# Moving one batch's preparation, the background's share and the queries' loads in a fused attention and expert kernel

## The chip, the cores and the metric

The kernel runs as one launch on 1 core of one Trainium2 chip. The metric is the device time of that launch in microseconds (us), from the first to the last instruction with what lies around it; lower is better. Engine names in profiles: PE is TensorE (PEld its weight loads), DVE is VectorE, ACT is ScalarE, POOL is GpSimd, SP is SyncE, which here only issues transfers. A trailing q (SPq) marks what an engine's sequencer does.

## What is computed

Input is x of shape (4, 2048, 256): four batches of 2048 tokens. Two blocks follow, each with a norm before and after and a residual.

```python
# block 1: attention with a triangular kernel instead of a softmax, 16 heads of 16 columns
h = layernorm(x)
q, k, v = h @ Wq.T + bq, h @ Wk.T + bk, h @ Wv.T + bv
z_q, z_k = q @ Wproj.T, k @ Wproj.T            # one number per head and token
ctx[i] = sum_j max(0, 1 - |z_q[i] - z_k[j]| / bandwidth[head]) * v[j] / T
x = x + layernorm(ctx)

# block 2: a shared feed-forward and 64 experts, two "halves" of two batches each in the kernel
h = layernorm(x)
shared = (silu(g) * u) @ shared_down * sigmoid(h @ shared_gate)      # g, u = h @ shared_gate_up
w, idx = top_k(softmax(h @ gate_w), 8);  w = w / sum(w)
# each expert takes its first 128 tokens in token order, over all 8192 tokens
y = sum over a token's experts of w * ((silu(g_e) * u_e) @ expert_down[e])
x = x + layernorm(y + shared)
```

The reference sorts z and uses prefix sums for the attention. The kernel evaluates the triangle directly.

## The kernel before

**The loop.** The attention is a hand-ordered loop of 1024 units, 256 for each of the four batches. A unit is one head and one row of 128 keys against all 2048 queries. It makes one score tile of 128 x 2048: `score` computes |q - k| on ScalarE (L1558), or on DVE when DVE has time to spare (L1553 and L1555), and then min(., 1) - 1 on DVE (L1562). `product` multiplies the tile with the values on TensorE (L1588); four units of four heads lie side by side in the array. `evict` takes a finished group of 8 heads out of PSUM. 64 units make a phase: four heads over all 16 rows of keys. The queries of a head are broadcast into a buffer of 128 x 2048 by `load_q` (L1539, two transfers of 512 KB). Before the change the first of the next phase's four heads is loaded at row 11 of 16 of the current phase, and the other three at the first three units of row 15. Query buffers, score tiles and finished groups share a pool of 13 big buffers, taken and given back in order; a score tile's buffer is free once TensorE has read it.

**The background.** All other work is a list of small tasks in the class `Background`: for each an engine, a cost in us, its dependencies and the buffers it takes and gives. After each unit of the loop, `step` emits the tasks whose dependencies are old enough, as long as an engine's cost stays within its share per unit, which is `CAP`. From the start of batch 2 (unit 512) the shares are larger (TensorE 0.88). If a task is needed and is still in the list, `flush` emits it at once. The order that results is fixed when the program is built. After the loop, `drain` emits what is left with a share of 1.0 for every engine.

**What the tasks are, in the order of the list before.** `prepare(i)` for batches 1, 2 and 3, one after the other: load x, norm, transpose, values to `v_d`, and the projection to z with 16 matrices from `m_d` (L436, L442). `finish(b)` once batch b's loop is done: `front` (context and x in, norm, gate), `shared` (the shared feed-forward, L573 and L602, a chunk of 512 tokens at a time) and `tail` (the routing); `stored[b]` lists the stores of the shared result into `y_d`. `finish(0)` waits for the end of `prepare(3)`. When batches 0 and 1 are routed, `all_experts` runs all 64 experts for their tokens: gather (L1041), two matmuls up, one down, and a scatter that adds into `y_d` (L1066).

**The tail.** After the loop: `front_last` for batch 3 (norm, gate, routing), the merge of the second half's tokens, `ranking`, and 15 items of one or two experts each (`item`; their scatters, L1258, add into two copies of `y_d` and wait for `stored[2]`, the stores of batch 2's shared result). What is left of the experts and of batch 2's shared chunks is interleaved, then `shared_last` (L911, L931) and `final`: load y (L1281), for the second half load its second copy and add it (L1288), for batch 3 add the shared result kept in SBUF (L1314), statistics (L1292), a power on POOL (L1298), norm on ScalarE (L1307), and an accumulating store from POOL (L1321). A branch for overflowing experts follows; it is not taken with these inputs.

Of the kernel before, what the change touches and what calls it, by code (L numbers as in the profile page):

```python
# [11 lines left out]
ALU = mybir.AluOpType  # L12
# [13 lines left out]
class Background:  # L26
# [3 lines left out]
           ("dve", "pe"): 1, ("dve", "sp"): 1, ("pool", "dve"): 2, ("dve", "pool"): 1, ("sp", "dve"): 4,  # L30
           ("sp", "pe"): 4, ("sp", "pool"): 4, ("sp", "act"): 5, ("sp", "sp"): 0, ("pool", "sp"): 1,
           ("act", "sp"): 1, ("pe", "sp"): 1}
    CAP = {"pe": 0.84, "dve": 0.65, "act": 0.30, "pool": 1.5, "sp": 2.0}

    def __init__(self, make):
        self.make = make
# [104 lines left out]
def sandwich_kernel(ctx: ExitStack, tc: tile.TileContext, x_in, wqT, bq, wkT, bk, wvT, bv, wprojT, log_bw,  # L141
                    gate_w, sgate_w, sgu_w, sd_w, egu_w, ed_w, out):
    nc = tc.nc
# [53 lines left out]
    def yrows(r0, n, j=0):  # L197

        p, r = part(r0)
        return rows(y_d[p + j], r, n)  # L200
# [25 lines left out]
    with ExitStack() as ph:  # L226
# [14 lines left out]
        def make(tag):  # L241
# [12 lines left out]
                return bigp.tile([P, T], F32, tag=tag, name=f"{tag}_{uid[0]}")  # L254
            return ps.tile([P, BK], F32, tag=tag, name=f"{tag}_{uid[0]}")

        NES, ess = 4, []
        bg = Background(make)
        bg.free["slot"] = [(f"s{i}", 0) for i in range(NSLOT)]
# [196 lines left out]
        def finish(b, after=()):  # L456
# [104 lines left out]
            def shared(c):  # L561
# [32 lines left out]
                for i2 in range(2):  # L594
# [15 lines left out]
                    if i2 == 0:  # L610
# [5 lines left out]
                    a = bg.add("pe", 1.07, lambda f=mmy: f(3), [a], put=acts if i2 == 1 else [], env=env)  # L616
                    yy += [e0, bg.add("dve", 0.45, lambda f=evy: f(1), [a, e0], put=[py], env=env)]
                free_act = a
                free_ys = bg.add("sp", 1.0, lambda ys=ys, r0=r0: nc.sync.dma_start(yrows(r0, CH, 0),
                                                                                   chunkview(env[ys])),  # L620
                                 yy, put=[] if b == NE else [ys], env=env)
# [645 lines left out]
        def final(env, c, deps, more=None, xd=(), tag=""):  # L1267
# [11 lines left out]

            def load(i):  # L1280
                nc.sync.dma_start(yv(i).rearrange("p (n f) -> p n f", n=CH), yrows(r0, CH, i))  # L1281
            l0 = l1 = bg.add("sp", 1.0, lambda: load(0), deps, get={yy: "big" if two else "slot"}, env=env)
            if two:
                l1 = bg.add("sp", 1.0, lambda: load(1), [l0])
            put = [yy]

# [21 lines left out]
                                         scale=rs()[:, i:i + 1])  # L1308
            a = bg.add("dve", 0.0, lambda: None, [l0, l1], get={sm: "v"}, env=env)
            put.append(sm)  # L1310
            if two:
                a = bg.add("dve", 1.25, add, [a])
            if more is not None:
                a = bg.add("dve", 1.25, lambda: nc.vector.tensor_tensor(yv(0), yv(0), more(), ALU.add),  # L1314
# [284 lines left out]
        with tc.manual_schedule():  # L1599
            for n in range(4):  # L1600
                load_q(n)
            for t in range(B * NU + 5):
# [7 lines left out]
                if t == 0:  # L1610
                    for c in range(2, NCH):
                        vts.append(values(env0, c, xt0[c], lambda i, c=c: v0[c * CH + i]))
                    zz = None
                    for q in range(4):
                        for k in range(KF):
                            ts, st = build(1, 4 * q, 4, k, "slot", "dve")
                            zz = accumulate(1, 4 * q, 4, k, ts, zz, st)
                            mst.append(st)
                    last[0] = project(env0, 0, zz, nk0, [1], None)
                    ends = [zz] + [v_[-1] for v_ in vts[1:]]  # L1620

                    def weights():
                        zrow = slot_tile()
                        nc.gpsimd.memset(zrow[:, :TW], 0.0)
                        for i in range(2):
                            nc.sync.dma_start(tab_d[i][TP[i]:TP[i] + P, :], zrow[:, :TW])
                            for j in range(1 + i):
                                nc.sync.dma_start(y_d[i + j][TP[i]:TP[i] + P, :], zrow[:, :F])
                        nc.sync.dma_start(gw[:, :, :E], gate_w.rearrange("(k p) e -> p k e", p=P))
                        with nc.allow_non_contiguous_dma(reason="one gate column"):  # L1630
                            nc.sync.dma_start(gw[:, :, E:E + 1], sgate_w.rearrange("(k p) e -> p k e", p=P))
                        nc.sync.dma_start(sgu, sgu_w.rearrange("(k p) f -> p k f", p=P))
                        nc.sync.dma_start(sd, sd_w.rearrange("(k p) f -> p k f", p=P))
                    bg.add("sp", 3.0, weights, [zz])
                    bg.add("pe", 0.0, lambda: None, ends, put=[("xT", c) for c in range(NCH)],
                           env=env0)
                    last[0] = [last[0]]
                    for i in range(1, B):
                        nks[i], last[i] = prepare(i, after=[last[i - 1]["end"]] if i > 1 else ts[-1:], mdeps=mst)
                if b == 0 and u in (28, 44):  # L1640
                    bg.flush(vts[u // 16 + 1])
                if u == 8 and b > 0:
                    finish(b - 1, after=[last[B - 1]["end"]])
                if u == 0 and b == B - 2:
                    bg.CAP = dict(bg.CAP, pe=0.88, dve=0.75, act=0.4)
                if t == B * NU - 12:
# [2 lines left out]
                if b == 0 and u == 200:  # L1649
                    zt_, z_tag = take("zeros")  # L1650
                    nc.gpsimd.memset(zt_[:, :CH * F], 0.0)
                    zfill = [(1, c) for c in range(NE * NCH, B * NCH)] + [(0, c) for c in range((B - 1) * NCH, B * NCH)]
                if b == 1 and u % 8 == 4 and zfill:
                    i, c = zfill.pop(0)
                    nc.sync.dma_start(yrows(c * CT, CH, i), chunkview(zt_))
# [9 lines left out]
                    bg.flush(last[b + 1]["v"][s:s + 1])  # L1665
                    nc.sync.dma_start(vtile(b + 1, s).rearrange("p a w -> p (a w)"), v_d[b + 1][s])
                if n + 4 < B * H:
                    if s == 11 and j == 0:
                        if ph_ == NU // UP - 1:
                            bg.flush(last[b + 1]["z"])  # L1670
                        if b == 0 and ph_ == 1:
                            bg.flush(last[0])
                        load_q(n + 4)
                    if s == NT - 1 and j < 3:
                        load_q(n + 5 + j)
                was = bg.spent["dve"]
                bg.step()
                spare[0] -= bg.spent["dve"] - was
# [35 lines left out]
            def second(deps, tag):  # L1714
                for c in range(NE * NCH, B * NCH):
                    l = c - (B - 1) * NCH
                    if l < 0:
                        final(env, c, deps, tag=tag)
                    else:
                        final(env, c, deps, lambda l=l: env["ys", l // 2][:, l % 2 * CH * F:(l % 2 + 1) * CH * F],  # L1720
# [69 lines left out]
```

## Time and profile before

| | us |
|---|---|
| median of 3 runs | 2340.97 (2337.17 to 2342.14) |
| profiled execution | 2339.91, of which the span in the trace is 2338.0 |
| loop, first score tile to last | 66 to 2035 |
| first half of the loop (units 0 to 511) | 963.2 |
| second half (units 512 to 1023) | 1005.3 |
| tail | 303 |

The mean granted clock of TensorE is 0.954. A profile page gives busy time, the number of instructions and, in groups, what ended the idle time before them: "112.8 <-DMA qb<-zq_d 57.5" says that the engine stood 112.8 us before these instructions, 57.5 of it until a transfer of queries had landed. Busy time of ScalarE counts overlapping instructions once: 959 score tiles of 1995 ns fill 1837.3 us, that is 1.92 us each. A wait is put down to what came last. An idle engine costs nothing unless others wait for it, and in this loop three engines are nearly full, so each can be the one that others wait for.

### The profile page before, as it was taken

The page shows a single profiled execution, that of the slowest core. Times are in us where ns is not written, and L with a number is a line of the kernel's source. Part 1 is how long each engine was busy: PE and PEld are TensorE (multiplying, and loading weights), DVE is VectorE, ACT ScalarE, POOL GpSimd, SP SyncE. Part 2 cuts the span into 40 slices and gives each one's busy share as a digit, 9 for nine tenths or more (in the row PEclk, how much of TensorE's full clock was granted, in tenths as well). Part 3 has the DMA queues.
Part 4 walks back from the last instruction along what each step waited for, and adds up shares of the span by engine and source line. Part 5 has one row for each costly group of instructions (what it writes and reads, how often), then busy time and mean ns, then how long its engine had stood idle before and what let it go on. Part 6 is the DMA issues. An engine that isn't in the chain of part 4 may idle for free. (4 is left out here: it accounts for less than half of the span.)

```text
span 2338.0 us, 32679 instructions
## 1 busy us (share of the span) xinstructions
PE 1952.5 (84%) x12552; PEld 687.2 (29%) x12552; DVE 1996.1 (85%) x3102; ACT 1966.8 (84%) x1269; POOL 490.4 (21%) x339
## 2 busy tenths in 40 slices
PE   7898979888799899677899887878888889987783
PEld 4332323222223222112222222223332223364342
DVE  4799999898999889999989998989999979886335
ACT  2899999898999998999999998989999989742213
POOL 1001010010120000003200003446553234442463
PEclk9999999999999999989999998999999999988897
DMA  4243534427351202142302014465544243355758
GB/s 127 91 133 120 184 103 153 151 88 264 117 162 64 91 19 70 37 147 69 112 19 81 28 54 122 114 186 151 174 121 136 57 134 90 102 177 147 177 124 197
DMA packets 195078, 274.32 MB, mean 117 GB/s; under 512 B 24833, under 2 KB 165505, under 8 KB 194145
## 3 DMA queue, kind: packets, MB, share of 16 engines
q1 hardware_dynamic: 165680, 235.33, 31.2%
q0 software_dynamic: 23824, 31.70, 8.3%
q10 hardware_dynamic: 5408, 5.11, 0.7%
q8 instruction: 101, 1.65, 0.3%
q14 instruction: 65, 0.52, 0.1%
HBM read 189.18 MB, written 82.90 MB: 116 GB/s over the span
## 5 line engine op out<-in xcount | busy, mean ns | idle before, releaser
L1558 ACT ACTIVATE hat<-qb,nk 128x2048 f32<-128x2048 f32 x959 | 1837.3, 1995 | 112.8 <-DMA qb<-zq_d 57.5
L1588 PE MATMUL pa<-hat,v 128*32 128x512 f32 x8192 | 1115.3, 620 | 284.4 <-DVE hat L1562 272.3
L1562 DVE TENSOR_SCALAR hat<-hat 128x2048 f32<-128x2048 f32 x1024 | 1230.3, 1223 | 97.2 <-ACT hat L1558 91.3
L1588 PEld LDWEIGHTS pa<-hat,v 128*32 128x32 f32 x8192 | 186.2, 110 | 900.0 <-DVE hat L1562 652.6
L1066 POOL DMA_INDIRECT y_d<-s,ix x64 | 147.8, 2309 | 286.7 <-DVE s L1064 145.4
L573 PE MATMUL k<-s,sgu 128*128 128x512 f32 x352 | 198.4, 651 | 0.0
L1041 POOL DMA_INDIRECT s<-tab_d,ix x64 | 106.0, 1657 | 327.6 <-DMA qb<-zq_d 259.0
L499 POOL TENSOR_TENSOR rsc<-rsc,mhalf 128x2 f32<-128x2 f32 x24 | 53.4, 2225 | 521.2 <-DVE rsc L498 521.0
L602 PE MATMUL k<-sd,s 128*128 128x256 f32 x384 | 113.7, 428 | 16.9 <-DVE s L589 7.4
L442 PE MATMUL k<-s,s 128*32 128x512 f32 x768 | 102.4, 592 | 0.0
L602 PEld LDWEIGHTS k<-sd,s 128*128 128x128 f32 x384 | 72.2, 205 | 86.4 <-issue 47.8
L573 PEld LDWEIGHTS k<-s,sgu 128*128 128x128 f32 x352 | 54.8, 192 | 136.3 <-issue 121.2
L305 POOL TENSOR_TENSOR rsa<-rsa,mhalf 128x4 f32<-128x4 f32 x16 | 30.8, 1925 | 290.9 <-DVE rsa L304 285.6
L1553 DVE TENSOR_SCALAR hat<-qb,nk 128x2048 f32<-128x2048 f32 x65 | 83.1, 1279 | 0.1
L1555 DVE TENSOR_SCALAR hat<-hat 128x2048 int32<-128x2048 int32 x65 | 79.9, 1229 | 2.2
L350 PE MATMUL k<-h,s 128*128 128x256 f32 x256 | 73.0, 413 | 0.0
L713 DVE MAX8 codes<-scT 128x8 f32<-128x1152 f32 (+2 forms) x48 | 63.4, 1321 | 0.2
L350 PEld LDWEIGHTS k<-h,s 128*128 128x128 f32 x256 | 45.4, 195 | 54.4 <-issue 48.6
L715 DVE MATCH_REPLACE8 scT<-codes,scT 128x1152 f32<-128x1152 f32 (+2 forms) x44 | 57.6, 1310 | 0.0
L607 DVE TENSOR_SCALAR s<-k,gt 128x256 f32<-128x256 f32 x48 | 22.8, 480 | 36.5 <-PE k L602 32.0
L442 PEld LDWEIGHTS k<-s,s 128*32 128x32 f32 x768 | 31.6, 138 | 54.0 <-issue 53.2
L1258 POOL DMA_INDIRECT y_d<-v,ix x28 | 39.9, 1426 | 23.5 <-DMA y_d<-s 7.9
(319 smaller groups left out, 1643.2 us busy)
## 6 DMA issues: line engine op xcount, KB each, us to landing
qb<-zq_d SPq DMA_DIRECT2D x128, 512.0 KB, 5.5
s<-m_d SPq DMA_DIRECT2D x48, 512.0 KB, 4.8
s<-_attn_hidden_states_dram SPq DMA_DIRECT2D x28, 512.0 KB, 5.5
v_d<-h SPq DMA_DIRECT2D x48, 192.0 KB, 2.6
v<-v_d SPq DMA_DIRECT2D x48, 192.0 KB, 2.5
h<-fn_expert_gate_up_w_dram SPq DMA_DIRECT2D x32, 256.0 KB, 3.5
s<-fn_expert_gate_up_w_dram SPq DMA_DIRECT2D x32, 256.0 KB, 2.8
b<-y_d SPq DMA_DIRECT2D x16, 512.0 KB, 9.3
```

The lines of the kernel that those rows point to most:

```text
L350: nc.tensor.matmul(env[pk][:, i * F:(i + 1) * F], lhsT=xv[:, k, o:o + P], rhs=wv[:, k, :], start=(k == 0), stop=(k == KF - 1))
L442: nc.tensor.matmul(env[pz][c * CR:(c + 1) * CR, :], lhsT=xv[:, r, :], rhs=env[mp][:, k * 2 * F:(k + 1) * 2 * F], start=(r == 0 and k == 0) ...
L573: nc.tensor.matmul(env[p_], lhsT=sgu[:, k, o:o + P], rhs=featview(env[xT])[:, k, :], start=(k == 0), stop=(k == KF - 1))
L602: nc.tensor.matmul(env[py][:, i * F:(i + 1) * F], lhsT=env[acts[f // 2]][:, o:o + P], rhs=sd[:, f, :], start=(f == 0), stop=(f == NI - 1))
L713: a = bg.add("dve", 1.25, lambda c8=c8: nc.vector.max(out=c8, in_=scT[:, :w]), ev + [a])
L1041: g = bg.add("pool", 1.3, lambda: nc.gpsimd.indirect_dma_start(out=xg(), out_offset=None, in_=tab_d[half][:, :], in_offset=bass.IndirectOf ...
L1066: s = bg.add("pool", 1.9, lambda: nc.gpsimd.indirect_dma_start(out=y_d[half][:, :], out_offset=bass.IndirectOffsetOnAxis(ap=iv(), axis=0), ...
L1553: nc.vector.tensor_scalar(ht, qb[n][0], k, None, ALU.add)
L1555: nc.vector.tensor_scalar(hi, hi, 0x7fffffff, None, ALU.bitwise_and)
L1558: nc.scalar.activation(ht, qb[n][0], AF.Abs, bias=k)
L1562: nc.vector.tensor_scalar(ht, ht, 1.0, 1.0, ALU.min, ALU.subtract)
L1588: nc.tensor.matmul(pa[k, c][32 * j:32 * j + 32, :], lhsT=vt[b, s].rearrange("p a w -> p (a w)")[:, h // 2 * VW + p * D:h // 2 * VW + p * D ...
```

## The change

Seven edits, made together:

1. TensorE's share for background in the first two batches goes from 0.84 to 0.72.
2. `prepare(3)` is added to the list behind `finish(0)`, when batch 1's loop has run 8 units, and waits for batch 0's last shared store. `finish(0)` now waits for the end of `prepare(2)`, `finish(1)` for that of `prepare(3)`.
3. The queries' loads of the next phase are spread: first head at row 12, second at the third unit of row 13, third and fourth at the first two units of row 15.
4. Chunks 2 and 3 of batch 2's shared result are not stored to `y_d`. They stay in two buffers in SBUF (`held`) until `final` adds them; `y_d` is filled with zeros there, so that two more zero fills run in batch 1. The copy for the branch that isn't taken is still stored.
5. In `final`, for these two chunks and batch 3's four, the second copy of y is no longer loaded by SP and added by DVE: an accumulating transfer on POOL's queue adds it to what the first load brought.
6. The first half's final loads are planned to take longer (`lat=9`), which moves the tasks that follow them in the order.
7. The scatters of the items wait for the two stores that are left in `stored[2]`.

```diff
-    CAP = {"pe": 0.84, "dve": 0.65, "act": 0.30, "pool": 1.5, "sp": 2.0}
+    CAP = {"pe": 0.72, "dve": 0.65, "act": 0.30, "pool": 1.5, "sp": 2.0}
...
+                if b == NE and c in LATE:
+                    held[c] = env, ys, yy
+                    free_ys = bg.add("sp", 1.0, lambda ys=ys, c=c: nc.sync.dma_start(rows(ysh_d, c * CT, CH),
+                                                                                    chunkview(env[ys])), yy)
+                    return
...
-            l0 = l1 = bg.add("sp", 1.0, lambda: load(0), deps, get={yy: "big" if two else "slot"}, env=env)
-            if two:
+            l0 = l1 = bg.add("sp", 1.0, lambda: load(0), deps, get={yy: "big" if two else "slot"}, env=env,
+                             lat=None if two else 9)
+            onto = two and more is not None and not tag
+            if onto:
+                l1 = bg.add("pool", 1.3, lambda: nc.gpsimd.dma_start(y3(), yrows(r0, CH, 1), accum_op=ALU.add), [l0], lat=4)
+            elif two:
                 l1 = bg.add("sp", 1.0, lambda: load(1), [l0])
...
-            if two:
+            if two and not onto:
                 a = bg.add("dve", 1.25, add, [a])
...
-                    for i in range(1, B):
+                    for i in range(1, B - 1):
                         nks[i], last[i] = prepare(i, after=[last[i - 1]["end"]] if i > 1 else ts[-1:], mdeps=mst)
...
                 if u == 8 and b > 0:
-                    finish(b - 1, after=[last[B - 1]["end"]])
+                    finish(b - 1, after=[last[max(last)]["end"]])
+                    if b == 1:
+                        nks[B - 1], last[B - 1] = prepare(B - 1, after=stored[0][-1:], mdeps=mst)
...
-                    zfill = [(1, c) for c in range(NE * NCH, B * NCH)] + [(0, c) for c in range((B - 1) * NCH, B * NCH)]
+                    zfill = [(1, c) for c in range(NE * NCH, B * NCH)] + [(0, c) for c in [NE * NCH + i for i in LATE] + list(range((B - 1) * NCH, B * NCH))]
...
-                    if s == 11 and j == 0:
+                    if s == 12 and j == 0:
...
-                    if s == NT - 1 and j < 3:
-                        load_q(n + 5 + j)
+                    if (s, j) in ((13, 2), (NT - 1, 0), (NT - 1, 1)):
+                        load_q(n + 5 + [(13, 2), (NT - 1, 0), (NT - 1, 1)].index((s, j)))
...
-                    if l < 0:
+                    if l < 0 and c - NE * NCH in held and not tag:
+                        e_, y_, d_ = held[c - NE * NCH]
+                        f_ = final(env, c, deps, lambda e_=e_, y_=y_: e_[y_][:, :CH * F], d_)
+                        bg.add("act", 0.0, lambda: None, [f_], put=[y_], env=e_)
+                    elif l < 0:
                         final(env, c, deps, tag=tag)
```

More of the change, by code (lines that the diff above doesn't have):

```diff
@@ L255, in make @@
             return ps.tile([P, BK], F32, tag=tag, name=f"{tag}_{uid[0]}")
+        LATE, held = (2, 3), {}
         NES, ess = 4, []
```

## The prediction

> **What bounds the kernel now.** I read the page first (shares, slices, groups), then ScalarE's waits in each half of the loop, then the timeline around the longest of those waits, and last the windows of the tail.
>
> ```profile
> PE 1952.5 (84%) x12552; PEld 687.2 (29%) x12552; DVE 1996.1 (85%) x3102; ACT 1966.8 (84%) x1269; POOL 490.4 (21%) x339
> PE   7898979888799899677899887878888889987783
> DVE  4799999898999889999989998989999979886335
> ACT  2899999898999998999999998989999989742213
> L1558 ACT ACTIVATE hat<-qb,nk 128x2048 f32<-128x2048 f32 x959 | 1837.3, 1995 | 112.8 <-DMA qb<-zq_d 57.5
> L1588 PE MATMUL pa<-hat,v 128*32 128x512 f32 x8192 | 1115.3, 620 | 284.4 <-DVE hat L1562 272.3
> L1562 DVE TENSOR_SCALAR hat<-hat 128x2048 f32<-128x2048 f32 x1024 | 1230.3, 1223 | 97.2 <-ACT hat L1558 91.3
> ```
>
> The loop of 1024 units runs from 66 to 2035 us and the tail from there to 2338. In the loop three engines are at eight or nine tenths together. ScalarE leads: 1837.3 us for its 959 score tiles and some 30 of background, against 1968. Its idle time, some 100 us, is what a change of order can win. Its causes by half:
>
> ```profile
> ACT hat L1558 <- PE pa L1588: 32.2, 34, 3.1
> ACT hat L1558 <- DMA qb<-zq_d: 6.9, 4, 3.5
> ...
> ACT hat L1558 <- DMA qb<-zq_d: 21.2, 11, 4.6
> ACT hat L1558 <- PE pa L1588: 17.4, 18, 2.5
> ACT s L1058 <- PE k L1051: 7.7, 7, 4.5
> ```
>
> The first two rows are the first half (80 to 1030 us), the rest the second. The 29.4 us that complete the page's 57.5 lie before 80 us, at the first loads of all, and are untouched. So 28.1 us are waits for the queries of the next phase, 49.6 are waits for TensorE to give a score buffer back. One queries' wait, on SP and on ScalarE:
>
> ```profile
> 1522.60 3.75 SPq L1539 DMA_DIRECT2D qb<-zq_d  x6
> 1531.06 2.00 ACT L1558 ACTIVATE hat<-qb,nk 128x2048 f32<-128x2048 f32 x1 [4.64 <-DMA qb<-zq_d]
> 1535.29 2.00 ACT L1558 ACTIVATE hat<-qb,nk 128x2048 f32<-128x2048 f32 x1 [2.06 <-DMA qb<-zq_d]
> 1538.51 3.90 ACT L1558 ACTIVATE hat<-qb,nk 128x2048 f32<-128x2048 f32 x2 [1.22 <-DMA qb<-zq_d]
> ```
>
> Three heads (six transfers of 512 KB) are issued in 3.75 us and needed from five units later, near 9 us; together they land 11.2 to 12.7 us after issue, against 5.5 in the median.
>
> ```profile
> 244.90:299.40 54.50, 54.50 (x504) 18.54 (x504) 50.99 (x48) 49.16 (x27) 0.00 (x0) 1.00 0.59 182
> 973.60:1029.60 56.00, 37.89 (x264) 7.33 (x264) 53.41 (x50) 52.77 (x29) 0.00 (x0) 0.88 0.28 86
> 2035.00:2306.40 271.40, 218.69 (x854) 131.75 (x852) 155.99 (x547) 72.52 (x146) 115.91 (x103) 0.88 0.66 166
> 2306.40:2338.00 31.60, 0.00 (x0) 0.00 (x0) 12.61 (x39) 9.03 (x18) 8.74 (x7) 0.56 0.70 109
> ```
>
> Windows (columns: PE, PEld, DVE, ACT, POOL busy, granted clock, DMA share, GB/s): units 96 to 127 fill TensorE wholly and ScalarE waits on it; units 480 to 511 have no background left and TensorE is two thirds busy. So the background is unevenly laid in the first half. In the tail TensorE ends at 2306.4. Who wrote y_d there:
>
> ```profile
> L619 SPq DMA_DIRECT2D y_d<-s x1: 359/359/359, 2201.0 to 2201.0; - x1
> L1258 POOL DMA_INDIRECT y_d<-v,ix x28: 1396/1404/1649, 2204.6 to 2271.9; - x28
> ```
>
> The 28 scatters of the last items stand until the last shared chunk of batch 2 is stored at 2201.0, then run back to back to 2273; the final norms follow, to the end.
>
> **The change part by part.** Counts come from the order of the two programs' instructions, durations from the rows.
>
> *Queries' loads.* The first head moves 4 units later (16 units ahead, still over 30 us). The second is issued 11 units ahead instead of 5; the third and fourth 6 instead of 5, and a burst is two heads, not three. Two heads at the burst's pace land near 12.7 x 2/3 = 8.5 us, needed at 6 x 1.92 = 11.5 us. I leave 6 of the 28.1 us: -22. The price: one big buffer more is held for 8 units in 64. ScalarE then meets the release wait one unit earlier; if the 49.6 us were spread evenly and doubled there, +6, at least 0. SP fills the buffers in order, so a load whose buffer TensorE still holds stops the value loads behind it. Value +2.
>
> *Smaller share.* By the planner's own costs (used here only for how evenly work is laid), background above 0.85 us of TensorE per unit, averaged over 8 units, stands at 110 of the first 512 places before and at 4 after; in the last 512 at 94 and 115 (batch 3's projection now ends at unit 540, under the larger share). No forced emission of late work is left in either order, so the smaller share makes nothing late at a phase's end. First half: 32.2 us of TensorE waits to some 15 (those at units 490 to 511, 3 us, come with an idle background and two engines at 95%): -17. Second half +4.
>
> *Batch 3's preparation.* It issues the same 4 input loads, 16 value stores, 16 matrix loads, 2 query stores on SP and 4 small powers on POOL, now behind batch 0's routing and shared work and ahead of batch 1's. Batch 1's finish starts at about unit 543 instead of 520, and the expert chain that follows is later by as much. When the loop ends, 6 expert gathers and 10 expert scatters are left instead of 2 and 5. An expert costs TensorE (25.2 + 41.1 + 39.5 + 22.6 + 21.9)/62 = 2.4 us (L1047, L1051, L1061), DVE 1.2, ScalarE 0.3. The loop sheds 4.5 x 0.3 = 1 us of ScalarE, and 66 score tiles go to DVE instead of 65: -2. The tail takes up 4.5 x 2.4 = 11 us of TensorE.
>
> Sum of the loop: -22 + 2 - 17 + 4 - 3 = -36. Not all of it comes: while ScalarE stands, TensorE and DVE catch up, and DVE is at 92% (886 of 963 us in the first half). Two thirds: **-24**, an estimate.
>
> *The tail.* Two of the chunks that the scatters waited for stay in SBUF, so no store at 2201.0 holds them; in the planner's new order the last of them stands 6 of its steps (a microsecond each, nominally) earlier. The held chunks cost two DVE adds of 1.23 us, and six adds of 1.22 (L1288) fall away: -5 us of DVE between scatters and end. Six second loads become accumulating transfers behind the first load: serial, about +10 us until the first chunk is ready, hidden while TensorE is still at the shared chunks, and +10 if it is not. Their price on the queue: the trace's row for an accumulating POOL transfer of 512 KB is L1321, landing in 8.5 us (5.7 to 11.1; it adds into DRAM, the new ones into SBUF), beside 8.6 for the plain SP load (L1281), so nothing. The Trainium skill (SBUF — State Buffer, section SBUF: two separate sides) speaks against it: while DVE runs an operation in a two-port mode, POOL can't write the descriptors of its own transfer, and a small one took about 3100 ns instead of 620. By that, 6 x 2.5 = 15 us on a POOL queue that also carries eight powers and eight output stores (29 us with the six issues, in 48). L1321 stands among the same DVE operations, so I take the row (2320 in the end; by the rule it would be 2335) and keep 15 for the range.
>
> TensorE's last work moves from 2306.4 by +11 to 2317 (loop end held fixed), less what fills its 53 us of idle. From there the new last chunk needs: eviction 1, add 1.2, four statistics 1.65, aggregation 0.8, power 1.3, shift 0.3, four norms 2.4, issue 1.3, landing 8.5: 18.5 us instead of the 31.6 of before, which DVE's eight norms and the loads filled. 2317 + 18.5 = 2336 against 2338. Against this +5 for the interleaving: output stores of the first half's norms now stand between the scatters on POOL. Value **+3**, from -10 to +20.
>
> The two zero fills more (12 to 14, on SP in batch 1) cover 16 units at one buffer less: nothing, at worst 1 us.
>
> Sum: 2339.9 (span 2338.0 and 1.9 around it) - 24 + 3 = 2319 for a profiled execution; the median of before is 1.1 above its profiled one: **2320 us**.
>
> **The rivals.**
> 1. *The gaps come back.* With queries on time ScalarE meets TensorE and DVE instead. For it: DVE at 92%, offloads that load DVE whenever it has spare. Against: in the windows above the uneven half has both a full and an empty TensorE. Loop -9, tail +3: 2335.
> 2. *The tail's end goes to TensorE and POOL (slower).* Five experts more, late in TensorE's order, push the last shared chunk: TensorE's end +11, and what follows it stays 31.6 instead of 18.5 because loads and accumulates are serial (+10): tail +21. It decides once the loop gives under about 16; with a loop of -11: 2351. For it: granted clock 0.88 in the tail, so work there is dearer than in the loop. Against: scatters no longer wait for 2201.0.
> 3. *The tail shrinks too.* The scatters go as soon as the items are done, and TensorE's 53 us of idle take up the experts. Tail -10, loop -30: 2301.
>
> **How the numbers follow.** Forecast 0.58 (2307 to 2334), rival 1 0.17, rival 2 0.13, rival 3 0.12. A difference under 0.2% (4.7 us) can't be told from none here. Rival 1 straddles that bound: half faster, half the same. Faster 0.58 + 0.12 + 0.08 = 0.78, same 0.09, slower 0.13. The range leaves out rival 2 and half of rival 3: 2301 to 2341.
>
> **What would show it.** In the profile after: ScalarE's waits for queries under 35 us in all (29 of them at the start), its waits for pa under 20 in the first half; no 32 units of the first half with TensorE full; the loop ending near 2011; a scatter of the items before 2195; TensorE's last work within 22 us of the end. Wrong if the loop ends after 2028, or if the time from its last unit to the end is over 313 us.

## The result and the profile after

The changed kernel takes 2362.98 us (median of 4 runs, 2359.7 to 2365.36), the kernel before beside it 2339.85 (4 runs): a ratio of 1.0109, 95% interval 1.0087 to 1.0132. It is slower by 1.1%; 2320 was predicted. The profiled execution took 2361.01 us, its span is 2359.2. From the page, shares, slices and the three largest groups (its other rows are left out):

```profile
PE 1961.6 (83%) x12552; PEld 693.7 (29%) x12552; DVE 1993.2 (84%) x3100; ACT 1965.6 (83%) x1268; POOL 498.9 (21%) x345
PE   7897887887888987888898997788888889777695
ACT  2899999999999999989999999889899989531213
L1568 ACT ACTIVATE hat<-qb,nk 128x2048 f32<-128x2048 f32 x958 | 1835.0, 1994 | 108.1 <-PE pa L1598 58.0
L1598 PE MATMUL pa<-hat,v 128*32 128x512 f32 x8192 | 1119.2, 621 | 287.1 <-DVE hat L1572 280.1
L1572 DVE TENSOR_SCALAR hat<-hat 128x2048 f32<-128x2048 f32 x1024 | 1227.6, 1222 | 81.3 <-ACT hat L1568 75.0
```

Ten lines were added above the score tiles, so L1558 of before is L1568 here. ScalarE's idle time before its score tiles hardly fell (112.8 to 108.1 us), but its cause is another: the waits for queries fell from 57.5 to 39.0 us, of which 30 lie before 80 us, and TensorE's late release of buffers leads with 58.0 (49.6 before). ScalarE's waits by half, as before (first two rows 80 to 1030 us, the rest from 1030 to 2050):

```profile
ACT hat L1568 <- PE pa L1598: 29.4, 31, 2.8
ACT hat L1568 <- DMA qb<-zq_d: 6.4, 3, 4.6
...
ACT hat L1568 <- PE pa L1598: 28.6, 27, 4.6
ACT s L1064 <- PE k L1057: 21.2, 13, 3.6
...
ACT hat L1568 <- DMA qb<-zq_d: 2.6, 2, 2.4
```

The queries' waits fell from 28.1 to 9.0 us. In the second half, waits for TensorE took their place: for score buffers 17.4 to 28.6, for the experts' matmuls (L1057) 7.7 to 21.2. Windows of the two halves of the loop and of the two parts of the tail, first of before (its tail was shown), then of after (columns as in the prediction):

```profile
66.40:1029.60 963.20, 835.72 (x5892) 257.81 (x5892) 886.35 (x1129) 914.88 (x498) 57.58 (x34) 0.97 0.35 114
1029.60:2034.90 1005.30, 849.76 (x5446) 267.62 (x5439) 912.68 (x1288) 954.57 (x584) 298.91 (x161) 0.97 0.37 106
```

```profile
65.50:1024.50 959.00, 809.94 (x5634) 243.36 (x5634) 887.74 (x1126) 915.16 (x498) 56.85 (x34) 0.97 0.34 110
1024.50:2038.40 1013.90, 869.89 (x5641) 280.58 (x5641) 907.94 (x1279) 952.37 (x579) 287.85 (x152) 0.96 0.38 107
2038.40:2342.20 303.80, 233.13 (x908) 139.87 (x907) 165.76 (x585) 79.34 (x162) 142.56 (x123) 0.86 0.70 164
2342.20:2359.20 17.00, 0.04 (x1) 0.00 (x0) 3.40 (x12) 2.91 (x6) 2.34 (x2) 0.58 0.39 58
```

258 matmuls left the first half and it became only 4 us shorter; 195 more run in the second half, with 20 us of TensorE, and it became 9 us longer in spite of the queries. The tail went from 303.1 to 320.8: TensorE needs 303.8 us to its last matmul instead of 271.5 (14.3 more of work and 18.0 more of idle), and 14.6 us came back after it (31.6 to 17.0). The scatters of the items and the stores of the shared result:

```profile
L1264 POOL DMA_INDIRECT y_d<-v,ix x28: 1408/1428/1667, 2183.3 to 2281.0; - x28
L625 SPq DMA_DIRECT2D y_d<-s x10: 359/371/397, 701.6 to 2104.3; - x10
```

The last store that scatters wait for is issued at 2104.3 instead of 2201.0, and the first scatter goes 144.9 us after the loop instead of 169.7, as meant. The last still goes 242.6 us after it, where before it was 237.0.

### The profile page after: what moved, and what is told of

Its sections match the earlier page's. It is cut to its first block, busy times and chain, and to the rows that moved or that the text cites. A ratio compares the mean times of both kernels' runs of the same rounds, so it can differ in the third digit from the quotient of the medians.

```text
span 2359.2 us, 32700 instructions
## 1 busy us (share of the span) xinstructions
PE 1961.6 (83%) x12552; PEld 693.7 (29%) x12552; DVE 1993.2 (84%) x3100; ACT 1965.6 (83%) x1268; POOL 498.9 (21%) x345
## 5 line engine op out<-in xcount | busy, mean ns | idle before, releaser
L1568 ACT ACTIVATE hat<-qb,nk 128x2048 f32<-128x2048 f32 x958 | 1835.0, 1994 | 108.1 <-PE pa L1598 58.0
L1072 POOL DMA_INDIRECT y_d<-s,ix x64 | 148.0, 2312 | 326.1 <-DVE s L1070 182.0
L603 PE MATMUL k<-sd,s 128*128 128x256 f32 x320 | 92.1, 414 | 5.9 <-DVE s L608 5.9
L603 PEld LDWEIGHTS k<-sd,s 128*128 128x128 f32 x320 | 56.8, 196 | 70.4 <-issue 47.5
L1064 ACT ACTIVATE s<-k 128x128 f32<-128x128 f32 x63 | 16.9, 269 | 40.4 <-PE k L1057 40.3
L1057 PEld LDWEIGHTS k<-s,h 128*128 128x128 f32 x256 | 35.3, 206 | 36.4 <-issue 31.5
```

The costliest lines, as they stand in the source:

```text
L603: nc.tensor.matmul(env[py][:, i * F:(i + 1) * F], lhsT=env[acts[f // 2]][:, o:o + P], rhs=sd[:, f, :], start=(f == 0), stop=(f == NI - 1))
L1072: s = bg.add("pool", 1.9, lambda: nc.gpsimd.indirect_dma_start(out=y_d[half][:, :], out_offset=bass.IndirectOffsetOnAxis(ap=iv(), axis=0), ...
L1568: nc.scalar.activation(ht, qb[n][0], AF.Abs, bias=k)
```

## The experiments

Each kernel was timed in rounds beside the kernel before on its own chip; ratios are to that, with 95% intervals. Halves (of the loop) and tail are those of the profiled execution, in us. "Left" are experts' scatters that are still to be issued when the loop ends, "unit" is where the first task of batch 1's finish is emitted; both follow from the order of the program. All kernels are written from the changed one with edits taken out, so the score tiles stand at L1568 in each but before. A profiled execution lies up to some 9 us from its kernel's median (in qb_only), so a few us between the halves of two kernels say nothing.

| kernel | ratio | halves | tail | left | unit |
|---|---|---|---|---|---|
| before | 1 | 963, 1005 | 303 | 5 | 520 |
| after | 1.0109 (1.0087, 1.0132) | 959, 1014 | 321 | 10 | 543 |
| qb_only | 0.9949 (0.9928, 0.9970) | 961, 984 | 303 | 5 | 520 |
| fin_only | 1.0015 (1.0006, 1.0024) | 967, 1004 | 300 | 5 | 520 |
| qb_fin | 0.9950 (0.9935, 0.9966) | 964, 986 | 301 | 5 | 520 |
| cap_only | 1.0027 (1.0017, 1.0037) | 968, 1001 | 307 | 6 | 520 |
| no_prep | 0.9976 (0.9961, 0.9990) | 959, 1001 | 305 | 6 | 520 |
| prep_only | 1.0109 (1.0077, 1.0142) | 961, 1013 | 318 | 8 | 539 |
| no_fin | 1.0071 (1.0046, 1.0095) | 961, 1008 | 319 | 10 | 543 |
| late_finish | 1.0102 (1.0068, 1.0136) | 965, 1009 | 321 | 10 | 543 |
| late_finish40 | 1.0115 (1.0092, 1.0139) | 965, 1002 | 333 | 14 | 560 |
| after_wait | 1.0069 (1.0037, 1.0102) | 961, 1008 | 315 | 10 | 543 |
| no_cap | 0.9986 (0.9972, 0.9999) | 958, 1002 | 304 | 8 | 539 |
| nocap_u31 | 1.0082 (1.0058, 1.0105) | 961, 1006 | 323 | 10 | 543 |
| share75 | 0.9956 (0.9943, 0.9969) | 965, 998 | 294 | 7 | 536 |
| repaired | 1.0041 (1.0027, 1.0056) | 960, 997 | 317 | 7 | 530 |
| qbfin_h2_96 | 1.0022 (1.0013, 1.0031) | 964, 1012 | 296 | 4 | 520 |

### The parts

**qb_only**: edit 3 alone.

```diff
-                    if s == 11 and j == 0:
+                    if s == 12 and j == 0:
...
-                    if s == NT - 1 and j < 3:
-                        load_q(n + 5 + j)
+                    if (s, j) in ((13, 2), (NT - 1, 0), (NT - 1, 1)):
+                        load_q(n + 5 + [(13, 2), (NT - 1, 0), (NT - 1, 1)].index((s, j)))
```

> Only the queries' loads are spread (edit 3); all else as before, and the order of the background's tasks is unchanged. Theory G (the wait moves): ScalarE's waits for queries after the start fall from 28 to under 10 us, its waits for TensorE (pa) rise by about as much, the loop stays within 5 us of 1968 and the time within 5 us of 2340. Rival S (spreading is a plain gain and something else ate it): loop -15 or more, time under 2327. Rival B (one buffer less costs more than the loads gave): time over 2345.

Measured: 2324.23 us, 0.9949. ScalarE's waits from 80 to 1030 us:

```profile
ACT hat L1568 <- PE pa L1598: 35.5, 33, 2.6
ACT hat L1568 <- DMA cx_d<-ct: 3.0, 2, 1.7
ACT hat L1568 <- DMA qb<-zq_d: 1.3, 1, 1.3
```

The loop ends at 2010.1 and the tail stays at 303.2. Queries' waits fall to 4.5 us (1.3 here, 3.2 in the second half), and what comes back in the first half is 3 us of waits for TensorE. The gain is the second half's, 22 us. The profiled execution is the fastest of its seven: by the medians the gain is 12 us, which is the prediction's 20 with its two thirds (13).

**fin_only** is edits 4 to 7 alone (chunks held in SBUF, accumulating second loads, longer planned loads), **qb_fin** is these with edit 3:

```diff
 # fin_only, against before: edits 4 to 7; qb_fin: edits 3 to 7
-        LATE, held = (), {}
+        LATE, held = (2, 3), {}
-                             lat=None)
+                             lat=None if two else 9)
-            onto = False
+            onto = two and more is not None and not tag
```

> Only edits 4, 5, 6: two shared chunks held in SBUF, second copy of y added by a transfer on POOL's queue, planned loads longer. The loop is that of before. Theory X: the tail is not longer than 303 + 3 us; the scatters start before 2190; time 2332 to 2343. Rival F: tail 312 or more, time 2349 or more.

> Edits 3 to 6: the queries' loads spread and the new final stage, without edits 1 and 2. If the parts add up: 2324 + 3 = 2327. If the new final stage gains once the loop is shorter: 2320 or less. If it loses: 2332 or more.

Measured: 1.0015 and 0.9950. Alone the edits of the tail cost 3 us; beside edit 3 they neither gain nor lose (0.9949 without them). The tail of qb_fin to TensorE's last matmul, and what follows:

```profile
2015.30:2300.10 284.80, 218.14 (x854) 131.65 (x852) 160.81 (x570) 78.24 (x158) 130.96 (x113) 0.86 0.69 161
2300.10:2316.70 16.60, 0.00 (x0) 0.00 (x0) 3.41 (x12) 2.90 (x7) 3.62 (x3) 0.61 0.65 95
```

With the same work on TensorE as before (218.1 us), its end comes 13.3 us later after the loop, and the chain behind it is 15.0 us shorter. The end was moved from one side of TensorE's last matmul to the other.

**prep_only** is edit 2 alone, **no_prep** is after without it, **no_fin** after without edits 4 to 7:

```diff
 # no_prep, against after
-                    for i in range(1, B - 1):
+                    for i in range(1, B):
...
-                    finish(b - 1, after=[last[max(last)]["end"]])
-                    if b == 1:
-                        nks[B - 1], last[B - 1] = prepare(B - 1, after=stored[0][-1:], mdeps=mst)
+                    finish(b - 1, after=[last[B - 1]["end"]])
```

> Only edit 2 (batch 3's preparation behind batch 0's finish). Theory M (the move is what costs, alone and in the mix): tail 315 or more against 303, loop up to 13 us longer, time 2352 to 2370. Rival C (the move costs only together with the smaller share): time under 2345.

> The changed kernel with edit 2 undone: batch 3's preparation runs again ahead of batch 0's finish. Theory X (the experts left over make the tail long): 6 expert scatters are left at the loop's end instead of 10, the tail falls from 321 us to 308 or less and the time from 2363 to 2340 to 2348. Rival F (the final stage's new transfers and held buffers make it long): tail still over 315, time over 2352.

> The changed kernel with edits 4, 5, 6 undone: batch 2's shared chunks are stored, the second copy of y is loaded by SP and added by DVE. Ten expert scatters are still left. Theory X: the tail stays within 5 us of 321, time 2357 to 2367. Rival F: tail 310 or less, time 2350 or less.

Measured: edit 2 alone costs as much as the whole change, 1.0109, and without it after would be faster than before, 0.9976. no_fin shows most of the loss (1.0071) without edits 4 to 7. So the loss is edit 2's, or needs it.

### How the move of batch 3's preparation costs

**late_finish** leaves the preparation where it was and only adds batch 1's finish to the list later, at unit 543, where it starts in after; **late_finish40** adds it at 560.

```diff
 # late_finish, against before (late_finish40: 48)
-                if u == 8 and b > 0:
+                if u == (31 if b == 2 else 8) and b > 0:
```

> Before, with batch 1's finish added at unit 543 instead of 520; batch 3's preparation stays where it was. 10 expert scatters and 6 gathers are left at the loop's end, as in the changed kernel. Theory L (the move costs because it makes the experts late): tail 317 to 323, time 2352 or more. Rival P (batch 3's preparation in its new place costs, by crowding what stands there): tail within 4 us of 303, time 2343 or less.

> The kernel before with batch 1's finish added to the list at unit 560 instead of 520 (late_finish added it at 543), and nothing else. 14 experts' scatters and 10 gathers are left when the loop ends, instead of 10 and 6 in late_finish and 5 and 2 before. Theory (each expert that is left for the tail costs about 3.5 us, since it stands in the in-order queues ahead of batch 3's routing and lengthens TensorE's tail): 9 experts more than before, about +32 us, tail near 333, ratio 1.013. Rival (the cost is a step, the routing is late by 8 to 9 us as soon as any expert stands ahead of it, and the loop's own loss does not grow): the same as late_finish, 2358, ratio 1.010, with the rows of the items known 101 us after the loop's end as there.

Measured: 1.0102 and 1.0115. One edit reproduces the loss: a finish that starts 23 units later. The experts wait for batch 1's routing, so five more of them are left when the loop ends. For the tail it makes little difference where the preparation is done: no_fin, with the preparation moved, has late_finish's background task by task from unit 560 to the end, and a tail of 319 beside 321. The tail of late_finish40 came out at 333.0, as expected of 3.5 us for each expert left, but its loop is 10 us shorter than late_finish's, so the time hardly grew: the tail came out as expected, the sum did not.

What do experts cost in the tail? The tail split at TensorE's last matmul, into TensorE's work and idle time up to it, and what follows:

| kernel | work | idle | after it |
|---|---|---|---|
| before | 218.8 | 52.7 | 31.6 |
| qb_fin | 218.1 | 66.7 | 16.6 |
| late_finish | 236.8 | 61.0 | 23.4 |
| after | 233.1 | 70.7 | 17.0 |
| after_wait | 227.8 | 70.1 | 17.2 |
| no_cap | 227.3 | 60.3 | 16.6 |
| nocap_u31 | 234.9 | 71.5 | 16.9 |
| share75 | 224.5 | 52.8 | 16.8 |

Late_finish has 18.0 us more of work than before and 8.3 more of idle; after has 15.0 and 4.0 more than qb_fin, which has the same edits of the tail. By lines, the experts' own matmuls (L1053, L1057, L1067) are most of that: 21.9 us in late_finish's tail against 9.9 before, 21.7 in after's against 10.1 in qb_fin's, some 12 us more. The loop, which is rid of that work, is no shorter for it in late_finish (it ends at 2039.8, before at 2034.9). But the experts' work alone doesn't make a tail long: no_cap's has 20.7 us of it and takes 304. The idle time runs from 53 to 72 us, by the order. How an expert can make idle time: POOL in the timeline, of before and then of after, around the moment at which the rows of the items become known (93 us after the loop before, 101 in after):

```profile
2094.38 1.56 POOL L1066 DMA_INDIRECT y_d<-s,ix  x1 [4.48 <-DVE scT L715]
...
2128.21 2.60 POOL L1217 DMA_INDIRECT v<-tab_d,ix  x1 [29.26 <-DVE ix L1139]
2131.11 0.98 POOL L1217 DMA_INDIRECT v<-tab_d,ix  x1 [0.30 <-issue]
```

```profile
2137.77 1.57 POOL L1072 DMA_INDIRECT y_d<-s,ix  x1 [11.20 <-DVE s L1070]
2143.03 1.55 POOL L1072 DMA_INDIRECT y_d<-s,ix  x1 [3.69 <-DMA b<-L_ffn_expert_down_w_dram]
2144.88 1.01 POOL L1223 DMA_INDIRECT v<-tab_d,ix  x1 [0.30 <-DVE b L929]
2150.19 1.58 POOL L1072 DMA_INDIRECT y_d<-s,ix  x1 [4.31 <-DMA y_d<-s,ix]
2152.08 1.01 POOL L1223 DMA_INDIRECT v<-tab_d,ix  x1 [0.30 <-issue]
```

Before, the experts' last scatter (L1066) goes at 2094, POOL stands 29 us, and the items' gathers go the moment the rows are there. In after, the experts' scatters (L1072) go until 2150. The last of these waited for the landing of the one before it (4.31 us), and the last three are 5 and 7 us apart; one stands between the first and the second gather of the items, and the second goes 113.7 us after the loop instead of 96.2. What this does to DVE and through it to TensorE, in the same moments:

```profile
2151.58 0.23 DVE L1240 TENSOR_TENSOR v<-v,b 128x64 f32<-128x64 f32 x1 [6.44 <-DMA v<-tab_d,ix]
2151.84 0.22 DVE L1241 TENSOR_REDUCE v<-v 128x1 f32<-128x64 f32 x1
2151.98 0.47 DVE L608 TENSOR_SCALAR s<-k,gt 128x256 f32<-128x256 f32 x1
...
2157.89 0.23 DVE L1240 TENSOR_TENSOR v<-v,b 128x64 f32<-128x64 f32 x1 [5.44 <-DMA v<-tab_d,ix]
```

```profile
PE k L1229 <- DMA v<-tab_d,ix: 8.2, 2, 7.4
PE pa L603 <- DVE s L608: 8.1, 2, 6.3
PE k L603 <- DVE s L608: 5.9, 2, 5.4
```

The second fence is TensorE's waits from 2138.4 to 2238.4. L1240 waits for an item's rows (6.44 and 5.44 us), and behind it in DVE's order stands L608, which empties a bank of batch 2's shared result that TensorE needs again. So one late gather holds DVE and, through it, TensorE. These three rows are 22.2 us of the 27.8 that TensorE stands in this stretch; before stands 25.1 us in the same 100, in shorter waits for other things, so a queue like this one explains how the idle comes about, not by itself that after's is larger.

**after_wait** takes one of these couplings away: in after, the gathers of the left-over experts wait until the rows of the items are known, so that the routing of batch 3 isn't behind them.

```diff
 # after_wait, against after
             mine = bg.q
+            for k in rest:
+                if k.eng == "pool" and k.cost == 1.3:
+                    k.deps.append(i_)
```

> The changed kernel, but the gathers of the experts that are left over wait until the items' rows are known, so that none stands among batch 3's routing on TensorE and POOL. Theory Q (standing in the order ahead of the routing is what costs): the routing ends 8 us earlier after the loop, tail 308 or less, time 2352 or less. Rival W (the experts' own work costs, wherever it stands): tail 315 or more, time 2357 or more.

Measured: the rows are known 92.8 us after the loop again, as before (100.7 in after), but the tail loses only 5.7 us of the 17.7 it had gained, and the median is 2350.99 (1.0069). The time fits theory Q (2352 or less) and the tail rival W (315 or more); the interval overlaps after's, so the gain isn't clear of noise. A late routing is at most a part of the loss: in no_cap the rows are known later than in after, at 106.4 us, and its tail is 304.

### The smaller share, and four units

**cap_only** is edit 1 alone; **no_cap** is after without it; **repaired** is no_cap with batch 1's finish not waiting for batch 3's preparation.

```diff
 # no_cap, against after (cap_only: the reverse, against before)
-    CAP = {"pe": 0.72, "dve": 0.65, "act": 0.30, "pool": 1.5, "sp": 2.0}
+    CAP = {"pe": 0.84, "dve": 0.65, "act": 0.30, "pool": 1.5, "sp": 2.0}
 # repaired, beside that
-                    finish(b - 1, after=[last[max(last)]["end"]])
+                    finish(b - 1, after=[last[max(last)]["end"]] if b != 2 else [])
```

> The kernel before with edit 1 alone (TensorE's share for background in the first two batches 0.72 instead of 0.84). Prediction's step: the first half loses 17 us of ScalarE's waits for TensorE, the second gains 4; two thirds of that, about -9 us, ratio 0.996. Theory now (the smaller share only moves background into the second half, where TensorE has no room): first half about 5 us shorter, second half about 14 us longer than before (1005), experts' scatters left at the end 6 instead of 5, tail within 3 us of 303; time +6 us, ratio 1.0025. Rival (edit 1 is harmless without the spread queries, because the second half then waits for queries anyway): second half within 4 us of 1005, ratio 0.998.

> After without edit 1 (share 0.84 as before; edits 2 to 7 stay). Planned: 8 experts' scatters and 6 gathers left when the loop ends, instead of 10 and 6. Theory (each scatter left costs about 3.5 us of tail, and the smaller share costs some 6 us beside that in the loop): tail near 314, time 2350, ratio 1.006. Rival (the smaller share is what kept the rest of the background out of the first half's way, so without it the loop grows): the first half 964 or more and the loop's end at 2040 or later, 2362 or more, ratio 1.011.

> After with 0.84 and with batch 1's finish not made to wait for batch 3's preparation (its list of tasks that it waits for is empty), though the preparation stays ahead of it in the list, as in edit 2. Planned: 7 scatters and 5 gathers left. Theory (what counts is how many experts are left, not where the preparation is done): tail near 310, time 2341, ratio 1.002, between qb_fin (5 left, 2323) and no_cap (8 left). Rival (the move of the preparation itself costs, by its loads and stores in the first half): as no_cap or slower, 1.006 or more.

Measured: alone the smaller share costs 6 us (1.0027), as expected in sum, though not where: the first half is not shorter (968), since its waits for queries grew from 6.9 to 19.9 us while those for TensorE fell from 32.2 to 25.9. In no_cap the theory of so many us for each expert left fell: 8 are left, as many as in prep_only, and the tail is 304, not 314. In repaired it fell the other way: 7 left and 317, not 310. And taking the smaller share out of after gave 29 us, five times its price alone.

The order says what the smaller share does besides: batch 3's preparation ends four units later, so batch 1's finish starts at unit 543 instead of no_cap's 539. **nocap_u31** has the first half of no_cap, but adds that finish at 543; from unit 560 to the end of the loop, and in the tail but for one task, the background is after's, task by task (between 543 and 560 a few tasks of the preparation differ). **share75** is after with a share of 0.75.

```diff
 # nocap_u31, against no_cap
-                if u == 8 and b > 0:
+                if u == (31 if b == 2 else 8) and b > 0:
 # share75, against after
-    CAP = {"pe": 0.72,
+    CAP = {"pe": 0.75,
```

> no_cap (share 0.84 in the first half, edits 2 to 7) with batch 1's finish added at unit 543 instead of 520, so that from unit 543 on the order of the background is after's, task by task, while the first half is no_cap's. Theory (what counts is the order that follows from when batch 1's finish starts: 10 experts' scatters left): tail near 320, time 2358 to 2363, ratio 1.010. Rival (the smaller share in the first half costs by itself when batch 3's preparation is moved too): as no_cap, 2334, tail near 304, ratio 0.999.

> After with a share of 0.75 instead of 0.72. Batch 1's finish then starts at unit 536, and 7 experts' scatters and 4 gathers are left when the loop ends. Theory (fewer experts left, shorter tail): tail near 308, time 2335 to 2340, ratio 1.000. Rival (the small share is what costs): 2360, ratio 1.010. Third (the order of the tail is new with each edit, and its length is not a function of the number left): anything between, with a tail that is not between no_cap's 304 and after's 321 by the count.

Measured: nocap_u31 2357.27 us (1.0082), share75 2328.63 (0.9956). The two parts of the tail, of no_cap and of nocap_u31:

```profile
2025.70:2313.30 287.60, 227.33 (x899) 137.21 (x897) 163.48 (x580) 79.39 (x162) 143.70 (x122) 0.88 0.74 171
2313.30:2329.90 16.60, 0.00 (x0) 0.00 (x0) 3.40 (x12) 2.91 (x6) 2.33 (x2) 0.56 0.27 39
```

```profile
2031.70:2338.10 306.40, 234.93 (x908) 141.10 (x907) 165.87 (x585) 79.41 (x163) 142.31 (x123) 0.86 0.71 163
2338.10:2355.00 16.90, 0.00 (x0) 0.00 (x0) 3.41 (x12) 2.88 (x6) 2.34 (x2) 0.60 0.34 50
```

Four units, 8 us of loop, at the start of one list make 23 us at the end: in the profile 6 in the loop and 19 in the tail, of which 7.6 are TensorE's work and 11.2 its idle. And a share nearly as small as after's, 0.75, gives one of the fastest kernels here: its finish starts at 536, the rows are known at 94.2 us, and its tail of 294 is the shortest of all, where its count of experts (7) stood for 308. What makes it so short is not shown; an early routing is not enough, since after_wait has its rows at 92.8 us. So a smaller share by itself is not the loss.

From these ratios the change can be walked through step by step. Edits 3 to 7 give -5.0 per mille (qb_fin). Edit 2 on top, without the delay by the smaller share, +3.6 (no_cap). The finish four units later, +9.6 (nocap_u31). What is left of the smaller share, +2.7 (after). The sum is +10.9 per mille: -12, +8, +22 and +6 us. It must come out so, as each step starts where the one before it ended; the last step is not clear of noise, and another way gives other parts (edit 2 alone +10.9, edits 3 to 7 on top of it -12.3, from prep_only to no_cap).

All six kernels whose finish starts at 543 or later are slow (1.0069 to 1.0115). Between 530 and 539 both kinds stand: no_cap and share75 are not slower than before, prep_only and repaired are. Repaired starts at 530 with its first chunk alone, the other three come within a unit of share75's, and its tail is 317. Prep_only, which has no_cap's background task by task until the loop ends, has a tail of 318 without edits 3 to 7. So the number left doesn't set the tail. Where the idle time of no_cap and nocap_u31 parts can be seen in TensorE's waits from 100 to 200 us after the loop, first no_cap, then nocap_u31:

```profile
PE pa L603 <- DVE s L608: 2.5, 1, 2.5
...
PE k L603 <- DVE s L608: 0.6, 1, 0.6
```

```profile
PE pa L603 <- DVE s L608: 12.1, 2, 7.7
PE k L1229 <- DMA v<-tab_d,ix: 8.1, 2, 7.1
PE k L603 <- DVE s L608: 1.4, 2, 0.9
```

L603 waits 3.1 us for L608 in no_cap, 13.5 in nocap_u31, 14.0 in after. In the last two an expert's scatter stands between the items' first two gathers, in no_cap none does. That isn't the whole reason: repaired has no such scatter either and waits 15.9 us there. The planner writes the tail anew from whatever is left, and its order there differs in many places; no run took these apart, so why the tail jumps between 539 and 543 stays open.

### Can the experts be finished in the loop instead?

**qbfin_h2_96** is qb_fin with a larger share for TensorE in the second half.

```diff
-                    bg.CAP = dict(bg.CAP, pe=0.88, dve=0.75, act=0.4)
+                    bg.CAP = dict(bg.CAP, pe=0.96, dve=0.75, act=0.4)
```

> Edits 3 to 7 without 1 and 2 (as qb_fin), and TensorE's share in the second half 0.96 instead of 0.88, so that less is left for the tail: 4 experts' scatters and some 9 us of TensorE's planned work less. Theory (work in the tail costs more than in the loop): tail 295, loop unchanged, 2317, ratio 0.992. Rival (TensorE has no room in the second half, ScalarE waits for it): loop 10 us longer, tail 8 shorter, 2325 or more, ratio 0.995 or more.

Measured: 2343.63 us (1.0022). The tail is 6 us shorter than qb_fin's and the loop ends 26 us later: the rival's way, but dearer than it said. The second half took 20.9 us more of TensorE's work and became 25.8 us longer, so it had no room for it. The fastest kernels stay qb_only, qb_fin and share75, at 0.995 to 0.996 of before; their intervals overlap.

## Why the prediction was wrong

The loop was to become 24 us shorter and the tail 3 us longer. In the profile the loop became 4 us longer and the tail 18. Of the six signs named for a right prediction, two came (the first scatter before 2195, TensorE's last work within 22 us of the end).

- **Queries' loads, -22 + 2.** Right. Their waits in the loop of after are 9.0 us (6 predicted) and alone the edit gave 12 us of median (25 us of loop in its fastest execution), where -22 + 2 and the two thirds make 13.
- **Smaller share, -17 in the first half and +4 in the second.** The first failed step. Evenly laid background was taken for less waiting: 29.4 us of TensorE waits are left in the first half (15 predicted), and 32 units in which TensorE hardly stands still (0.4 us, units 208 to 239, from 453.3 to 506.0) exist as before, only elsewhere. Alone the edit was to gain about 9 us and costs 6. I costed the sharing of the first half and not its sum: 36 matmuls go over into the second half in cap_only, and in after their delay is passed on along the list.
- **Batch 3's preparation, -3 in the loop and +11 of TensorE in the tail.** The step that failed most: after is 31 us slower than no_prep, which leaves this edit out (1.0109 and 0.9976). The count was right (10 scatters left), and so was the work: 14.3 us more instead of 11, of which the experts' matmuls are 11.8. What I did not cost is the second half of the loop, which took up 195 matmuls (+20 us of TensorE; waits for score buffers and experts +25 us), although five experts left it. Nor did I cost what the start at unit 543 does to the order of all that follows: late_finish, which has only that, loses 1.0 per cent. And of the tail's new work nothing went into TensorE's 53 us of idle, as the +3 for the tail had supposed for a part.
- **Two thirds of the loop's sum.** Wrong in sign. The loop ended at 2038.4, not near 2011; after 2028 was named as the mark of a wrong prediction.
- **Tail, +3.** +17.7. Of its parts the end behind TensorE's last matmul was right, 18.5 predicted and 17.0 measured, and so was that scatters no longer wait for a store (first at 2183.3). The end of TensorE was not: +32 instead of +11: 14.3 of work, and 18.0 of idle. Of the idle 14 stand in qb_fin too, so they come with edits 4 to 7; I had booked the 13 us that these win behind TensorE's end, and not that they are paid ahead of it.
- **Accumulating transfers on POOL at nothing.** Half right. Issuing one takes 1.26 to 2.65 us on POOL, median 1.47 (six, L1292), near the row L1321 that I took (1.3). The 3100 ns of the Trainium skill (SBUF — State Buffer, section SBUF: two separate sides) don't show; that is no test of its rule, since no run here tells which of DVE's operations in this stretch are in a two-port mode. But the row's landing time hid what six back to back do to the transfer engines (below).
- **The rivals.** Rival 2 named the tail's place and a time near it (2351, and a tail of +21), and was given 0.13. Its mechanism is in part what happened: experts in TensorE's and POOL's queues. It had what follows TensorE's end at 31.6 and the loop at -11; measured were 17.0 and +4, so that its numbers come near is in part luck. Against it I had put that scatters no longer wait, which was true and did not decide. Rival 1's gaps did not come back with the queries on time: in qb_only the waits for score buffers are 35.5 and 14.3 us in the two halves, 49.8 together, before 49.6.

## What to carry to other kernels

When a step is moved in a list of background work, price what stands behind it in the list before the step itself: here the step cost some 8 us, and four units of delay for its successor cost 23 us. Work that leaves a stage for the tail is not free: in after none of it went into the tail's idle time, and the loop that shed five experts was no shorter. Nor does a count of what is left forecast the tail: no_cap carried nearly as much expert work as nocap_u31, and its tail was 19 us shorter. Emptying the first half of 258 matmuls gained 4 us, and 21 us more of TensorE in the second made it 26 us longer. So the sum of an engine's work in each stage is to be compared, not only how evenly it lies.

## What the runs showed of the hardware that was not expected

Six accumulating transfers on POOL's queue from DRAM into SBUF filled the transfer engines at little over half the rate of the plain loads before them. The last chunks' y in after, in slices of 0.3 us from 2282 to 2294 (plain loads on SP's queue) and in slices of 0.5 us from 2296 to 2316 (accumulating second loads on POOL's queue, 98.6% of 16 engines); both rows are the busy share in tenths and the rate:

```profile
DMA  0009999079999763899999999999999999999999
GB/s 0 0 0 75 147 109 119 34 259 382 389 352 174 150 55 61 280 362 375 379 376 375 348 358 379 382 362 358 358 348 352 352 345 352 348 345 352 348 348 345
```

```profile
DMA  9999999999999999999999999999999999999999
GB/s 356 344 346 356 348 348 297 242 236 231 213 203 205 195 207 201 197 199 193 199 199 199 197 197 195 199 197 199 199 193 197 203 197 199 191 203 197 199 203 189
```

With all engines busy, 350 GB/s against 197. Six chunks of 512 KB are 3.1 MB: 16 us instead of 9. It is the adding and not POOL's queue: in after's trace a packet of 1 KB takes 46 ns in the median on SP's queue and 102 ns in POOL's accumulating transfers, while the packets of POOL's plain gathers (5 KB, 196 ns) keep the pace of SP's packets of 4 KB (159 ns): 26 bytes per ns in both. DVE stood 6.9 us for the first of them in after (L1324 waiting for y), with the products that TensorE's last matmuls need in the same queue; the same wait is 6.0 to 7.7 us in qb_fin, no_cap, nocap_u31 and share75, so it isn't what sets after apart. The accumulating output stores of before reached the same rate (up to 208 GB/s from 2310 to 2325), but were issued 5 us apart, and their landing time didn't show what six back to back would cost.
